# The first scan's convolution as four diagonal matrix products, with a longer ring of row tiles and later stores

## The chip, the core and the metric

The kernel runs on one core of a Trainium2 chip. The core has five engines that run side by side and meet at semaphores: TensorE (PE in the profile; its weight loads are shown apart as PEld), VectorE (DVE), ScalarE (ACT), GpSimd (POOL) and SyncE (SP), which here issues DMAs. Each engine works through its own instruction stream in order. The metric is the device time of one execution, in microseconds (us); lower is better. Three executions of the kernel before took 3533.27, 3534.64 and 3535.41 us, median 3534.64.

## What is computed

The input is 32 sequences of 256 tokens with 256 channels. The result is `x + ffn(cond(x))`: a selective scan, then two layers of local attention and a gated feed-forward. The change lies in `cond`. Cut to what matters:

```python
xr, gate = split(x @ W_in.T)                       # 512 channels each
xr = xr + t_emb[:, None, :]
xc = depthwise_conv(xr, W_conv, 4 taps, 3 zeros in front) + b_conv
xc = silu(xc)
xn = layernorm(xc) * ln_g + ln_b
Bm, Cm, dt = split(xn @ W_xproj.T)
dt = tanh(dt @ W_dt.T + b_dt) * 0.01
Ad, Bd = 1 - dt * tanh(A_log), Bm * min(norm(xn), 1)
for t in range(256):                               # the scan
    h = clip(h * Ad[t] + Bd[t] * xn[t], -10, 10)   # 16 states x 512 channels
    y[t] = Ct[t] . h
return (y + D * xn) * silu(gate) @ W_out.T
```

Each of the 512 channels is convolved with four taps of its own: `xc[c, t] = sum over k of W_conv[c, k] * xr[c, t + k - 3]`.

## The kernel before

The 32 sequences go through in four groups of eight. A group's scan holds its state in a tile of 128 partitions (16 states x 8 sequences) by 512 channels, and takes 256 steps in eight chunks of 32. The scan of group 0 runs by itself (`alone` in the code); those of groups 1 to 3 run beside the attention and feed-forward of the group before. The program between is one long interleaving.

**A step** (L715) is one VectorE instruction: the new state `h` is the old one plus the row `xrep`, clipped. Before it, `scale_row` (L704) multiplies the row by `beta` on ScalarE, and before that the row has to be there, copied to all 16 states. That is done in two ways. For 24 of 32 rows `load_rows` (L684) issues a DMA on SP, 256 KB, from a DRAM copy of the normalised activations (`xnd`). For the other eight (`by_tensor`, two of every eight steps) `spread_rows` (L689) makes it on TensorE (`bx`) from a tile `xq`, which `load_skip` (L738) loads. Both kinds end in a tile of the pool `xp`, tag `xrep`, six buffers. The read-out `y` (L725) is a product on TensorE for each step; four steps write four separate quarters of the same bank.

**The convolution** of the next chunk runs around the start of the current one, for each of four blocks of 128 channels. `project` (L397) forms `ps_in` on TensorE. `conv_in` (L462) adds the condition on VectorE and so writes `xr`, with three tokens carried over from the chunk before in front (runs of 35 for each sequence), and starts the sum `acc` on GpSimd (L480, the first tap and the bias). `conv_taps` (L488) adds three more taps on VectorE (L491). `conv_th` (L496) applies Silu on ScalarE in the first scan; in the later scans tanh is used and `conv_out` finishes it on VectorE. Then follow `raw_sums` (L517), the transposition (`norm_turn`), the norm and `norm_out` (L591), which stores `xn` to `xnd`.

**Beside the first scan** TensorE also projects the inputs of groups 1 to 3: 48 units `ps_a` (`ahead_project`, L423), copied by ScalarE and stored by `ahead_put` (L442), to be read back by the later scans. The weights of the first layer are loaded in this time as well.

**Order.** Each piece of work is entered in an agenda with `at(slot, function, ...)`, where slot `c * 32 + t` is that of step `t` of chunk `c`; `scan_slots` (L935) emits the slots in order, and within one slot first the entries before `agendas.append({})` (L896), then those after it. The framework then writes each engine's stream at compile time: what was emitted first has precedence, but an instruction that isn't ready in its model lets later ones pass. So a stream isn't strictly in slot order: the first weight load of the first layer, emitted in slot 100, is issued at 18.90 us, long before the first step. Once written, a stream is worked through in order.

The slots that matter here, `s0` being the first slot of a chunk: `conv_in` at `s0 - 38 + 2 ch`, `conv_taps` one and `conv_th` two slots later; `norm_out` at `s0 - 17` and `s0 - 13`; `load_skip` at `s0 - 9` and `s0 + 7`; `load_rows` six slots, `spread_rows` four and `scale_row` two ahead of the step.

Of the kernel before, what the change touches and what calls it, by code (L numbers as in the profile page):

```python
# [10 lines left out]
FP = mybir.dt.float32  # L11
BF = mybir.dt.bfloat16
I32 = mybir.dt.int32
AF = mybir.ActivationFunctionType
ALU = mybir.AluOpType
# [4 lines left out]
P = 128  # L20
# [3 lines left out]
DI = 512  # L24
NC_ = DI // P
NS = 16
GB = 8
CH = 32
# [7 lines left out]
TAPS = 4  # L36
# [37 lines left out]
def kernel(  # L74
# [29 lines left out]
    nc = tc.nc  # L104
# [33 lines left out]
    wc_sb = loaded(w_conv, [P, NC_, TAPS], "wc_sb")  # L138
    bconv_sb = loaded(b_conv, [P, NC_], "bconv_sb")
# [5 lines left out]
    ident = const.tile([P, P], FP, tag="ident", name="ident")  # L145
# [17 lines left out]
    for j in range(NJ):  # L163
# [20 lines left out]
        out=mask_t[:, 0:W], in_=mask_t[:, 0:W], compare_op=ALU.is_ge, fill=MASKED_LOW,  # L184
# [3 lines left out]
        out=mask_t[:, W : 2 * W], in_=mask_t[:, W : 2 * W], compare_op=ALU.is_ge,  # L188
# [35 lines left out]
    def program(ctx, exact):  # L224
# [11 lines left out]
        def bank(pool, tag, name):  # L236
            return pool.tile([P, DI], FP, tag=tag, name=name)
# [141 lines left out]
        def group_scan(g):  # L379
# [14 lines left out]
            def at(s, what, *args):  # L394
                agendas[-1].setdefault(s, []).append(partial(what, *args))
# [66 lines left out]
            def conv_in(c, ch):  # L462
                if ch == 0:
                    ck[c]["carry"] = sm.tile(
                        [P, NC_, GB, TAPS - 1], FP, tag="carry", name="carry"
                    )
                    ck[c]["xc"] = sp.tile([P, NC_, GB * CH], FP, tag="xc", name="xc")
                ps = ck[c].pop(("ps", ch))
                xr = sp.tile([P, GB, TAPS - 1 + CH], FP, tag="xr", name="xr", bufs=2)
                if c == 0:  # L470
                    nc.gpsimd.memset(xr[:, :, 0 : TAPS - 1], 0.0)
                else:
                    nc.gpsimd.tensor_copy(xr[:, :, 0 : TAPS - 1], ck[c - 1]["carry"][:, ch])
                nc.vector.tensor_add(
                    xr[:, :, TAPS - 1 :],
                    ps.rearrange("p (b t) -> p b t", b=GB),
                    bc(cond_sb[:, ch, b0 : b0 + GB], 2, CH),
                )
                acc = sp.tile([P, GB, CH], FP, tag="acc", name="acc", bufs=2)
                nc.gpsimd.tensor_scalar(  # L480
                    acc, xr[:, :, 0:CH], wc_sb[:, ch, 0:1], bconv_sb[:, ch : ch + 1],
                    ALU.mult, ALU.add,
                )
                if c < NCH - 1:
                    nc.gpsimd.tensor_copy(ck[c]["carry"][:, ch], xr[:, :, CH:])
                ck[c]["xr", ch] = xr, acc

            def conv_taps(c, ch):  # L488
                xr, acc = ck[c]["xr", ch]
# [6 lines left out]
            def conv_th(c, ch):  # L496
                acc = ck[c]["xr", ch][1]
                if alone:

                    ck[c].pop(("xr", ch))  # L500
                    nc.scalar.activation(
                        ck[c]["xc"][:, ch], acc.rearrange("p b t -> p (b t)"), AF.Silu
                    )
                    return
                th = sp.tile([P, GB * CH], FP, tag="th", name="th", bufs=2)
                nc.scalar.activation(th, acc.rearrange("p b t -> p (b t)"), AF.Tanh, scale=0.5)
                ck[c]["th", ch] = th
# [81 lines left out]
                nc.gpsimd.tensor_add(xn, xn, lnb_sb)  # L589

            def norm_out(c, j):  # L591
                xn = ck[c].pop(("xn", j))
                nc.sync.dma_start(out=ck[c]["xnd"][j * P : (j + 1) * P], in_=xn)
                sq = sp.tile([P, DI], BF, tag="th", name="sq_x", bufs=2)
                nc.scalar.activation(
                    sq, xn, AF.Square, accum_out=ck[c]["ss"][:, j : j + 1]
                )

            def length(c):
# [81 lines left out]
            def by_tensor(t):  # L681
                return alone and t % (2 * NQ) < XR

            def load_rows(c, t):  # L684
                xr = xp.tile([P, DI], FP, tag="xrep", name="xrep")
                ck[c]["rep", t] = xr
                nc.sync.dma_start(out=xr, in_=bc(rows(c)[:, t, :], 0, NS))

# [14 lines left out]

            def scale_row(c, t):  # L704
                if by_tensor(t):
                    ck[c]["rep", t] = xp.tile([P, DI], FP, tag="xrep", name="xrep")
                bx = ck[c]["rep", t]
                scaled = nc.scalar.activation(  # L708
                    bx, ck[c].pop(("bx", t), bx), AF.Copy, scale=ck[c]["beta"][:, t : t + 1]
                )  # L710
                if not alone:

                    tc.keep_in_program_order(scaled)
# [136 lines left out]
            rep_w = []  # L850
            at(-1, start)
            if alone:
                at(-30, spread_weights)
                constants(at)
            for c in range(NCH):
# [2 lines left out]
            for c in range(NCH):  # L858
                s0 = c * CH
                for hb in range(CH // TB):  # L860
                    s = s0 + hb * TB
                    for i in range(NI):
                        at(s + 4 * i + 5, read_out, c, hb, i)
                    at(s + 21, gated, c, hb)
                    at(s + 25, out_gate, c, hb)
                    at(s + 11, skip, c, hb)
                for ch in range(NC_):
                    at(s0 - 38 + 2 * ch, conv_in, c, ch)
                    at(s0 - 37 + 2 * ch, conv_taps, c, ch)
                    at(s0 - 36 + 2 * ch, conv_th, c, ch)  # L870
                    if not alone:
                        at(s0 - 35 + 2 * ch, conv_out, c, ch)
                for ch, s in enumerate((13, 16, 17, 18)):
                    at(s0 + s + 2, gate_th, c, ch)
                    if not alone:
                        at(s0 + s + 4, gate_out, c, ch)
                at(s0 - 25, raw_copy, c)
                at(s0 - 24, raw_turn, c)
                for j in range(NJ):
                    s = s0 - 26 + 4 * j  # L880
                    at(s + 2, norm_stats, c, j)
                    at(s + 5, norm_shift, c, j)
                    at(s + 5, norm_apply, c, j)
                    at(s + 6, norm_affine, c, j)
                    at(s + 9, norm_out, c, j)
                at(s0 - 11, length, c)
                at(s0 - 9, figures, c)
                at(s0 - 7, figures_in, c)
                at(s0 - 6, decay_th, c)
                at(s0 - 5, decays, c)  # L890
                at(s0 - 4, put_c, c, 0)
                at(s0 + 4, put_c, c, 1)
                for d in range(KM):
                    at(s0 + 45 + 2 * d, copy_y, c, d)
                    at(s0 + 46 + 2 * d, put_y, c, d)
            agendas.append({})  # L896
            for c in range(NCH):
                s0 = c * CH
                at(s0 - 43 if alone else s0 + 6, load_x, c)
                if alone:  # L900
                    for ch in range(NC_):
                        at(s0 - 40 + 2 * ch, project, c, ch)
                else:
                    for i in range(2):
                        at(s0 - 44 + 2 * i, load_projected, c, i)
                for ch, s in enumerate((13, 16, 17, 18)):
                    at(s0 + s, project, c, NC_ + ch)
                at(s0 - 27, raw_sums, c)
                for j in range(NJ):
                    at(s0 - 26 + 4 * j, norm_turn, c, j)  # L910
                at(s0 - 8, figures_out, c)
                for t in range(CH):
                    if not by_tensor(t):
                        at(s0 + t - 6, load_rows, c, t)
                    if by_tensor(t) and t % XR == 0:
                        at(s0 + t - 4, spread_rows, c, t)
                    at(s0 + t - 2, scale_row, c, t)
                for hb in range(CH // TB):
                    s = s0 + hb * TB
                    at(s - 9 if alone else s + 7, load_skip, c, hb)  # L920
                    at(s + 23, out_turn, c)
                for d in range(KM):
                    at(s0 + 43 + 2 * d, project_y, c, d)

            if alone:
                n = (NG - 1) * NCH * 2
                for u in range(n):
                    s = -30 + u * (NCH * CH) // n
                    at(s - 5, ahead_load, u)
                    at(s, ahead_project, u)  # L930
                    at(s + 2, ahead_copy, u)
                    at(s + 4, ahead_put, u)
            return agendas

        def scan_slots(groups):  # L935
# [758 lines left out]
```

## Time and profile before

| | |
|---|---|
| median of three runs | 3534.64 us |
| profiled execution: its own time / its span | 3538.39 / 3536.6 us |
| busy over the span: PE, DVE, ACT, POOL | 3415.9, 2682.6, 2031.8, 1625.6 us |
| first step of the first scan | 48.7 us |
| first attention product (L991) | 471.3 us |
| mean granted TensorE clock | 0.992 |

The profile is one execution recorded by the hardware. A row of a group gives line, engine and operation, output and inputs with their shapes, the number of instructions, then busy time in us and the mean of one in ns, and last the idle time of the engine just before them with what ended it. A row of a wait gives who waited for whom, us in total, how many times, and the longest. A row of the timeline gives start, duration, engine, line, operation and, in brackets, the idle time before it. Names are those of the program's tiles; L491 is line 491. Busy times of one group are a union, so that instructions side by side are not counted twice, while means are from each instruction's start to its modelled end.

### The profile page before, as it was taken

The page shows a single profiled execution, that of the slowest core. Times are in us where ns is not written, and L with a number is a line of the kernel's source. Part 1 is how long each engine was busy: PE and PEld are TensorE (multiplying, and loading weights), DVE is VectorE, ACT ScalarE, POOL GpSimd, SP SyncE. Part 2 cuts the span into 40 slices and gives each one's busy share as a digit, 9 for nine tenths or more (in the row PEclk, how much of TensorE's full clock was granted, in tenths as well). Part 3 has the DMA queues.
Part 4 walks back from the last instruction along what each step waited for, and adds up shares of the span by engine and source line. Part 5 has one row for each costly group of instructions (what it writes and reads, how often), then busy time and mean ns, then how long its engine had stood idle before and what let it go on. Part 6 is the DMA issues. An engine that isn't in the chain of part 4 may idle for free.

```text
span 3536.6 us, 56518 instructions
## 1 busy us (share of the span) xinstructions
PE 3415.9 (97%) x19580; PEld 2255.2 (64%) x19580; DVE 2682.6 (76%) x5177; ACT 2031.8 (57%) x3663; POOL 1625.6 (46%) x1587
## 2 busy tenths in 40 slices
PE   7999989999999999999999999999999999999999
PEld 4545335666666666666666666666666777777777
DVE  5888898878787778888888888888787655555563
ACT  4666656666666665666656665666566444444442
POOL 4433456544454555544455455544444434333441
PEclk9999999999999999999999999999999999999999
DMA  7787765544455545444354555444444212011111
GB/s 206 215 218 217 199 172 149 137 115 137 132 138 137 155 141 149 137 115 139 115 143 124 150 145 149 135 118 129 121 140 119 62 37 62 13 31 36 37 28 38
DMA packets 487195, 436.65 MB, mean 123 GB/s; under 512 B 247155, under 2 KB 326516, under 8 KB 486772
## 3 DMA queue, kind: packets, MB, share of 16 engines
q1 hardware_dynamic: 402450, 420.94, 42.2%
q10 hardware_dynamic: 84450, 12.01, 2.1%
q8 instruction: 157, 2.57, 0.3%
q14 instruction: 138, 1.13, 0.1%
HBM read 384.06 MB, written 47.19 MB: 122 GB/s over the span
## 4 chain that ended last, share of the span: by engine, by line
PE 60%; DVE 18%; DMA 8%; POOL 5%; ACT 5%; issue 3%; SPq 0%; ACTq 0%; DVEq 0%; POOLq 0%
PE ps_qkv L991 13%; PE pa L1402 13%; DVE h L718 7%; PE po_f L1429 6%; DMA xrep<-xnd 5%; PE ps_wo L1047 4%; PE y L730 4%; PE ov L1282 3%; PE sc L1227 3%; PE ps_out L810 3%; PE ps_in L401 2%; PE tr_qk L1036 2%; DVE acc L491 2%; PE rs L1264 2%; PE ps_raw L520 2%
## 5 line engine op out<-in xcount | busy, mean ns | idle before, releaser
L718 DVE CUSTOM_DVE_ANT_0 h<-h,xrep,lim 128x512 f32<-128x512 f32 x1024 | 916.7, 895 | 148.1 <-ACT xrep L708 104.4
L708 ACT ACTIVATE xrep<-xrep,beta 128x512 f32<-128x512 f32 x960 | 672.8, 720 | 292.0 <-DMA xrep<-xnd 192.3
L991 PE MATMUL ps_qkv<-qkv,res 128*128 128x512 f32 x1536 | 715.1, 601 | 20.3 <-DVE xd L781 9.5
L1402 PE MATMUL pa<-hT,w 128*128 128x256 f32 (+1 forms) x2816 | 674.3, 382 | 6.0 <-DVE zT L801 6.0
L1402 PEld LDWEIGHTS pa<-hT,w 128*128 128x128 f32 (+1 forms) x2816 | 517.0, 188 | 146.1 <-issue 42.4
L1015 POOL TENSOR_TENSOR rot<-rot,swp 128x512 f32<-128x512 f32 x256 | 346.1, 1352 | 496.4 <-DVE swp L1012 462.0
L991 PEld LDWEIGHTS ps_qkv<-qkv,res 128*128 128x128 f32 x1536 | 281.7, 191 | 304.3 <-issue 246.8
L1021 POOL TENSOR_TENSOR rn<-ss,neg_half 128x8 f32<-128x8 f32 x256 | 458.9, 1793 | 0.0
L730 PE MATMUL y<-h,ly 128*32 128x512 f32 x2048 | 343.8, 606 | 16.3 <-DVE h L718 14.3
L1429 PE MATMUL po_f<-ag,w 128*128 128x256 f32 x1280 | 307.2, 387 | 3.9 <-DVE fo L1440 2.8
L1420 DVE SCALAR_TENSOR_TENSOR ag<-pa,b_sb,ag 128x256 f32<-128x256 f32 x320 | 151.3, 473 | 204.9 <-ACT ag L1413 204.8
L1429 PEld LDWEIGHTS po_f<-ag,w 128*128 128x128 f32 x1280 | 235.8, 190 | 68.3 <-DVE pT L1255 12.9
L1004 ACT ACTIVATE sq<-ps_qkv,tiny 128x512 f32<-128x512 f32 x256 | 172.2, 685 | 178.2 <-PE ps_qkv L991 118.7
L1413 ACT ACTIVATE ag<-pa,b_sb 128x256 f32<-128x256 f32 x320 | 150.3, 470 | 208.9 <-PE pa L1402 205.9
L1354 POOL TENSOR_TENSOR rstd<-ve,neg_half 128x2 f32<-128x2 f32 x64 | 46.2, 722 | 484.9 <-DVE ve L1352 484.9
L1047 PE MATMUL ps_wo<-oT,wo 128*128 128x256 f32 x1024 | 231.6, 379 | 0.0
L1007 DVE TENSOR_TENSOR rot<-ps_qkv,rc_sb 128x512 f32<-128x512 f32 x256 | 174.2, 680 | 67.4 <-ACT sq L1004 65.8
L491 DVE SCALAR_TENSOR_TENSOR acc<-xr,wc_sb,acc 128x256 f32<-128x256 f32 x384 | 184.8, 503 | 49.0 <-POOL acc L480 48.3
L1012 DVE TENSOR_TENSOR swp<-ps_qkv,rs_sb 128x256 f32<-128x256 f32 x512 | 191.8, 416 | 27.6 <-POOL rot L1015 27.5
L1047 PEld LDWEIGHTS ps_wo<-oT,wo 128*128 128x128 f32 x1024 | 194.5, 190 | 27.2 <-ACT xrep L708 0.8
L1239 ACT ACTIVATE pT<-sc 128x512 f32<-128x512 f32 x384 | 201.7, 601 | 14.8 <-PE sc L1227 12.7
L1227 PE MATMUL sc<-qT,kT 64*128 64x128 f32 (+2 forms) x2304 | 197.6, 331 | 12.6 <-DVE swp L1012 8.8
(161 smaller groups left out, 5379.1 us busy)
## 6 DMA issues: line engine op xcount, KB each, us to landing
xrep<-xnd SPq DMA_DIRECT2D x960, 256.0 KB
rb<-inv SPq DMA_DIRECT2D x128, 256.0 KB
xnd<-xn SPq DMA_DIRECT2D x64, 256.0 KB
qkv<-in_wqkv_dram SPq DMA_DIRECT2D x24, 512.0 KB
ahead<-xs_a SPq DMA_DIRECT2D x48, 256.0 KB
xp<-ahead SPq DMA_DIRECT2D x48, 256.0 KB
xd<-xnd SPq DMA_DIRECT2D x192, 64.0 KB
w<-in_w_dram SPq DMA_DIRECT2D x80, 128.0 KB
```

Source lines behind the costliest of these rows:

```text
L491: nc.vector.scalar_tensor_tensor(acc, xr[:, :, k : k + CH], wc_sb[:, ch, k : k + 1], acc, ALU.mult, ALU.add,)
L708: scaled = nc.scalar.activation(bx, ck[c].pop(("bx", t), bx), AF.Copy, scale=ck[c]["beta"][:, t : t + 1])
L718: nc.vector._custom_dve(TENSOR_ADD_SAT, out=h_new, in0=state["h"], in1=bx, s0=ck[c]["lim"][:, 0, t : t + 1], s1=ck[c]["lim"][:, 1, t : t + 1],
L730: nc.tensor.matmul(ck[c]["y", hb][32 * q : 32 * q + 32, :], ly[hb % 2][:, 32 * t : 32 * t + 32], ck[c].pop(("h", hb * TB + t)), start=(i = ...
L991: nc.tensor.matmul(ps, res[b][:, k, t0 : t0 + W], wt["qkv", a][:, k], start=(k == 0), stop=(k == KM - 1),)
L1015: nc.gpsimd.tensor_add(rot, rot, swp)
L1021: nc.gpsimd.tensor_tensor(rn, ss, neg_half, ALU.pow)
L1047: nc.tensor.matmul(po[:, d], wt["wo", 0][:, c, d * P : (d + 1) * P], oT[:, c, :], start=(c == 0), stop=(c == NC_ - 1),)
L1227: nc.tensor.matmul(banks[r][k0 : k0 + mk, i, q0:q1], kT[rows, i0 + i, kw * W + k0 : kw * W + k0 + mk], qT[rows, i0 + i, kw * W + q0 : kw * ...
L1239: nc.scalar.activation(p, banks[r], AF.Exp)
L1402: nc.tensor.matmul(dst[x], wt["w1", m][:, k, x], self.h[:, k], start=(k == 0), stop=(k == KM - 1),)
L1429: nc.tensor.matmul(self.po[:, d], wt["w2", 0][:, m, d * P : (d + 1) * P], self.ag[m], start=(m == 0), stop=(m == len(MCH) - 1),)
```

## The change

It has four parts, all for the first scan (`alone`) of the usual branch of the program.

1. The sum `acc` on GpSimd and the three taps on VectorE are dropped. At the start `taps_diagonal` writes for each block of channels and each tap a 128 x 128 matrix with the tap's weights on its diagonal (16 ScalarE activations of the identity with a scale for each partition). `conv_products` then forms the convolution as four accumulating products on TensorE in a PSUM bank, with `xr` shifted by one token as the moving operand, one slot after `conv_in`. The Silu reads that bank and adds the bias.
2. The rows' tiles come from a ring of ten: six of `xp` and four in tiles that the attention uses later (`qT`, `kT`, `rb`, `v`). The diagonals lie in such tiles too (`oT`, `hn`, `hT`).
3. `load_rows` is entered eight slots ahead of the step, not six.
4. The store of `xn` is parted from `norm_out` (`norm_put`) and entered two slots later; the store of a projected half (`ahead_put`) four slots later.

```diff
-                acc = sp.tile([P, GB, CH], FP, tag="acc", name="acc", bufs=2)
-                nc.gpsimd.tensor_scalar(
-                    acc, xr[:, :, 0:CH], wc_sb[:, ch, 0:1], bconv_sb[:, ch : ch + 1],
-                    ALU.mult, ALU.add,
-                )
+                acc = None
+                if not alone:
...
+            def taps_diagonal(ch):
+                if ch == 0:
+                    t = ap_.tile([P, 2, TAPS, P], FP, tag="oT", name="taps", bufs=1)
+                    state["taps", 0], state["taps", 1] = t[:, 0], t[:, 1]
+                elif ch > 1:
+                    state["taps", ch] = ap_.tile(
+                        [P, TAPS, P], FP, tag=("hn", "hT")[ch - 2], name="taps", bufs=1
+                    )
+                for k in range(TAPS):
+                    nc.scalar.activation(
+                        state["taps", ch][:, k], ident, AF.Copy, scale=wc_sb[:, ch, k : k + 1]
+                    )
+
+            def conv_products(c, ch):
+                xr, _ = ck[c]["xr", ch]
+                ps = bank(ps_w, "w", "cv")[:, 0 : GB * CH]
+                for k in range(TAPS):
+                    nc.tensor.matmul(
+                        ps.rearrange("p (b t) -> p b t", b=GB),
+                        state["taps", ch][:, k],
+                        xr[:, :, k : k + CH],
+                        start=(k == 0),
+                        stop=(k == TAPS - 1),
+                    )
+                ck[c]["xr", ch] = xr, ps
...
-                        ck[c]["xc"][:, ch], acc.rearrange("p b t -> p (b t)"), AF.Silu
+                        ck[c]["xc"][:, ch], acc, AF.Silu, bias=bconv_sb[:, ch : ch + 1]
...
+            def norm_put(c, j):
+                nc.sync.dma_start(
+                    out=ck[c]["xnd"][j * P : (j + 1) * P], in_=ck[c].pop(("xn", j))
                 )
...
+            def row_tile():
+
+                n = state["rows"] = (state.get("rows", -1) + 1) % (6 if exact else 10)
+                if not alone or n < 6:
+                    return xp.tile([P, DI], FP, tag="xrep", name="xrep")
+                tag = ("qT", "kT", "rb", "v")[n - 6]
+                t = ap_.tile(
+                    [P, 2, DI], FP, tag=tag, name="xrep", bufs=2 if tag == "v" else 1
+                )
+                return t[:, 0]
...
+                for ch in range(NC_):
+                    at(-41 + ch, taps_diagonal, ch)
...
-                    at(s0 - 37 + 2 * ch, conv_taps, c, ch)
+                    if not alone:
+                        at(s0 - 37 + 2 * ch, conv_taps, c, ch)
...
+                    at(s + (11 if alone else 9), norm_put, c, j)
...
+                        at(s0 - 37 + 2 * ch, conv_products, c, ch)
...
-                        at(s0 + t - 6, load_rows, c, t)
+                        at(s0 + t - (8 if alone and not exact else 6), load_rows, c, t)
...
-                    at(s + 4, ahead_put, u)
+                    at(s + 8, ahead_put, u)
```

`load_rows` and `scale_row` take their tile from `row_tile()` instead of the pool.

More of the change, by code (lines that the diff above doesn't have):

```diff
@@ L478, in conv_in @@
                 )
-                acc = sp.tile([P, GB, CH], FP, tag="acc", name="acc", bufs=2)
-                nc.gpsimd.tensor_scalar(
-                    acc, xr[:, :, 0:CH], wc_sb[:, ch, 0:1], bconv_sb[:, ch : ch + 1],
-                    ALU.mult, ALU.add,
-                )
+                acc = None
+                if not alone:
+                    acc = sp.tile([P, GB, CH], FP, tag="acc", name="acc", bufs=2)
+                    nc.gpsimd.tensor_scalar(
+                        acc, xr[:, :, 0:CH], wc_sb[:, ch, 0:1], bconv_sb[:, ch : ch + 1],
+                        ALU.mult, ALU.add,
+                    )
                 if c < NCH - 1:
@@ L591, in norm_out @@
             def norm_out(c, j):
-                xn = ck[c].pop(("xn", j))
-                nc.sync.dma_start(out=ck[c]["xnd"][j * P : (j + 1) * P], in_=xn)
+                xn = ck[c]["xn", j]
                 sq = sp.tile([P, DI], BF, tag="th", name="sq_x", bufs=2)
@@ L596, in norm_out @@
                     sq, xn, AF.Square, accum_out=ck[c]["ss"][:, j : j + 1]
+                )
+            def norm_put(c, j):
+                nc.sync.dma_start(
+                    out=ck[c]["xnd"][j * P : (j + 1) * P], in_=ck[c].pop(("xn", j))
                 )
@@ L682, in by_tensor @@
                 return alone and t % (2 * NQ) < XR
+            def row_tile():
[5 more added lines that the diff above has]
+                    [P, 2, DI], FP, tag=tag, name="xrep", bufs=2 if tag == "v" else 1
+                )
+                return t[:, 0]
             def load_rows(c, t):
-                xr = xp.tile([P, DI], FP, tag="xrep", name="xrep")
+                xr = row_tile()
                 ck[c]["rep", t] = xr
@@ L705, in scale_row @@
                 if by_tensor(t):
-                    ck[c]["rep", t] = xp.tile([P, DI], FP, tag="xrep", name="xrep")
+                    ck[c]["rep", t] = row_tile()
                 bx = ck[c]["rep", t]
```

## The prediction

> **What bounds the first scan.** The change touches the first scan alone: head (0 to 48 us), scan proper, then a mixed stage from about 471 us in which TensorE is never short of work (295.0 of 300 us busy between 600 and 900 us, clock 1.00). What the first scan saves or costs is therefore passed on to the end one for one, and I looked there only. I read first busy time by stretch, one row per chunk of 32 steps (columns: stretch, its length, busy us of PE, PEld, DVE, ACT, POOL, then the granted clock, DMA share, GB/s):
>
> ```profile
> 96.00:145.00 49.00, 44.45 (x203) 25.52 (x203) 43.43 (x76) 31.87 (x58) 21.13 (x29) 0.98 0.80 220
> 145.00:193.00 48.00, 44.89 (x201) 23.70 (x201) 41.98 (x72) 30.67 (x59) 19.80 (x26) 0.96 0.79 216
> 193.00:242.00 49.00, 45.72 (x204) 24.66 (x203) 40.91 (x74) 31.48 (x58) 17.93 (x25) 0.95 0.81 222
> 48.00:387.00 339.00, 316.85 (x1403) 171.81 (x1402) 287.59 (x503) 219.30 (x404) 132.27 (x173) 0.96 0.80 216
> ```
>
> A chunk takes some 48.4 us, in which TensorE is busy 45 us, VectorE 42 us and the DMA engines 80%. None is idle enough to be ignored. Next, the groups of instructions in the seven chunks between 48 and 387 us:
>
> ```profile
> L718 DVE CUSTOM_DVE_ANT_0 h<-h,xrep,lim 128x512 f32<-128x512 f32 x221 | 207.3, 938 | 27.9 <-ACT xrep L708 18.7 <-DVE h L718 2.0 <-PE y L730 0.3
> L428 PE MATMUL ps_a<-xa,w_in_sb 128*128 128x256 f32 x344 | 92.0, 413 | 3.6 <-DMA xa<-in_xT_dram 3.6
> L730 PE MATMUL y<-h,ly 128*32 128x512 f32 x441 | 84.0, 606 | 2.6 <-DVE h L718 2.5
> L401 PE MATMUL ps_in<-xg,w_in_sb 128*128 128x256 f32 x216 | 60.2, 413 | 2.4 <-DMA xg<-in_xT_dram 2.2 <-ACT xrep L708 0.2
> L491 DVE SCALAR_TENSOR_TENSOR acc<-xr,wc_sb,acc 128x256 f32<-128x256 f32 x81 | 40.6, 501 | 8.1 <-POOL acc L480 8.1
> L480 POOL TENSOR_SCALAR acc<-xr,wc_sb,bconv_sb 128x256 f32<-128x256 f32 x28 | 28.2, 1008 | 59.1 <-DVE xr L474 56.3 <-ACT xs_a L439 2.0 <-ACT xrep L708 0.8
> ```
>
> L491 and L480 are what goes. The means of the PE rows (413 ns) are latencies; what a matmul costs in a queue is read from TensorE's timeline, from start to start:
>
> ```profile
> 143.85 3.20 PE L428 MATMUL ps_a<-xa,w_in_sb 128*128 128x256 f32 x8
> 150.21 1.99 PE L428 MATMUL ps_a<-xa,w_in_sb 128*128 128x256 f32 x8
> 152.13 1.13 PE L695 MATMUL bx<-xq,rep_w 32*128 32x512 f32 x4
> 153.19 1.05 PE L730 MATMUL y<-h,ly 128*32 128x512 f32 x4
> ...
> 154.71 1.04 PE L730 MATMUL y<-h,ly 128*32 128x512 f32 x2 [0.47 <-DVE h L718]
> ...
> 172.00 1.89 PE L401 MATMUL ps_in<-xg,w_in_sb 128*128 128x256 f32 x8
> 173.82 1.07 PE L730 MATMUL y<-h,ly 128*32 128x512 f32 x8
> 174.81 1.99 PE L401 MATMUL ps_in<-xg,w_in_sb 128*128 128x256 f32 x8
> ```
>
> One call of a 128x128x256 product leaves two records, so x8 is four calls: 1.82 to 1.92 us from start to start, 1.86 in the mean. Four read-outs y cost 1.0 us when they run side by side (x8) and 1.0 us for each lot when split (x4, x2). At 143.85 the same eight records took 3.20 us: a low clock after a stop.
>
> **Where TensorE stops**, waits in the same 339 us:
>
> ```profile
> PE bx L695 <- ACT xrep L708: 6.2, 3, 2.4
> PE bx L695 <- DMA xq<-xnd: 4.9, 4, 1.8
> PE ps_a L428 <- DMA xa<-in_xT_dram: 3.6, 4, 1.3
> PE ps_st L620 <- DVE rhs L611: 2.5, 4, 0.9
> SPq L687 <- DVE h L718: 42.2, 49, 3.9
> SPq L593 <- POOL xn L589: 6.0, 6, 2.2
> ```
>
> The stops sit at the chunk boundaries. At 188.5 us ScalarE has stood 3.67 us for a row whose load SP had issued only at 183.4; the decay's activation behind it came late, VectorE waited 2.0 us for that, TensorE 1.9 us for the bank of bx.
>
> **Part 1, the convolution leaves VectorE and GpSimd.** In the 339 us 81 L491 go, 40.6 us, and their 8.1 us of waiting for L480: VectorE needs 239 us instead of 288. That alone would allow 339 - 48.7 = 290 us if nothing else were late. GpSimd loses 28 us. L718's mean is 938 ns against a minimum of 785, because it lengthens beside GpSimd's passes (1.70 us at 208.88 beside L760); L480 is one of these passes. I put no gain on it (0 to 3 us).
>
> **Part 2, it comes to TensorE.** Four calls per channel and chunk, the shape of L401: 1.86 us for each of 27 channel-chunks in the stage (81/3) = 50.2 us. That xr is read in runs of 32 out of 35 isn't shown by a row of this shape; between 0 and +10% I take 0, since weights and columns are those of L401. Weight loads overlap (25 of 48 us busy). ScalarE's 32 Silu keep their cost (L501: 412 ns; bound -0.05 to +0.2 us each when read from PSUM, L439's copy of 512 columns takes 0.58). Sixteen diagonals on ScalarE: 128x128 lies between L645 (128x32, 0.31 us) and L501 (0.41), 5 to 7 us, in the first 10 us, where ScalarE is busy 1.5 us. The first xr is ready at 12.8 us; cost 0, and up to 3 us if they delay the weight DMAs that ScalarE issues.
>
> The stage's ledger for TensorE, by counts and starts: ps_a 43 x 1.87 = 80.4, ps_in 27 x 1.83 = 49.4, y 55 x 1.0 = 55, bx 28.5 x 1.06 = 30.2, ps_out 12 x 1.88 = 22.6, ps_raw 14, transposes 13.3, ps_st 3.5: 268.4 us. The other 70.6 of 339 us are: idle 22.2; 29 for split y (84.0 - 55); 12.7 for the clock (4% of 316.9); 7 left over. With the convolution the ledger is 318.6, so TensorE becomes the bound, and the result hangs on how much of the 70.6 survives.
>
> A rule stands against that reading. The Trainium skill (Perfetto Trace Analysis, Identifying the Most-Contended Engine) holds that TensorE's headroom isn't judged by matmul busy time but by the weight loads' busy share. That is 51% here (171.8 of 339) and would leave ample room, so that VectorE's 290 us would count: -49 us. The row decides otherwise: from 161 to 183 us TensorE's matmuls start without a gap at the very spacing that the bound needs, and the sum of spacings is 79% of the stage. I take the row.
>
> **Part 3, ring of ten and loads two slots earlier.** A load waited for the step six rows back, of its own slot (42.2 us of SP's waiting on L718). Now the tile is that of ten rows back, stepped two slots before. Two slots are 3.0 us, which covers most of the 3.67 us stop. So bx<-ACT (6.2) goes, and with it low clock. For the clock the skill (TensorE: Matmul & The Clock Gate, Why this matters for your kernels) warns of gaps over some 3 us; the gaps here are 1.9 and 2.4 us, so that by the rule nothing is lost now, yet the row shows 0.66 between 190 and 200 us. By the rule 0 us is to be regained, by the row 12.7; I take the row. DMA share would be 0.82 at the forecast length: no bound (slices of 0.99 occur), but more loads stand in front of xq, whose lateness (4.9 us) I keep.
>
> **Part 4, stores later.** xnd's store loses its place before two slots of row loads and ahead's before four; SP's waits for them (6.0 and, for xs_a, 11.8 us) stop blocking loads. Readers: xq two slots later. The stores preceded the xq loads by 8.0 us (226.57 to 234.62), so 3 us less is covered; without that cover each of seven boundaries would cost up to 3 us. The projected halves are read from slot 212, far behind.
>
> **Sum.** When TensorE is always behind, y come in fours and it stops rarely: between 600 and 900 us it idles 1.7% at clock 1.00, and y cost 1.19 us per four. Full batching gives 0, that row 10.5 us; I take 4, since here all of TensorE's work is queued. Of the 7 left over I keep 4. (318.6 + 8)/0.983 = 332 us, **-7** against 339 (ends: 324 with nothing kept, 373 with 54 of the 70.6 kept). After 387 us neither convolution is on TensorE; ScalarE waits 13.9 us for rows in that chunk but L718 hardly for ScalarE: -3 (-6 to +1). Head: 0 (-2 to +3). Total -10 on the profiled span, 3536.6 to 3526.6; that run took 3538.39, the runs' median is 3534.64, so **3525 us**; own range 3510 to 3533.
>
> **Rivals.** *Wash*: y at 1.19 us and all 7 kept: (318.6 + 17.5)/0.983 = 342, +3 - 3: 3535 us. For it: that is the only saturated row there is. *Slower*: the diagonal products wait on TensorE. They stand at the boundary, each behind its xr addition, which VectorE does between steps; the spread rows bx stand behind them in order, and the steps behind bx; ScalarE's Silu now waits for TensorE too, with the row scalings behind it. At 0.9 us a channel, 27 x 0.9 = 24 us on a full engine, plus 10 for y left split: +34 - 10 = 3559 us. It decides from about 0.4 us a channel. For it: L474 came 2 us after its ps_in at 188.1; against it: three slots (4.5 us) lie between. *VectorE was all*: the weight loads' reading is right, 3534.6 - 49 = 3486 us.
>
> **Chances.** A change under 0.2% (7 us) can't be told from none. Forecast 0.42 (0.06 of it within 7 us), wash 0.20 (0.16 within, 0.04 above), slower 0.30, VectorE 0.08. Faster 0.44, same 0.22, slower 0.34. Range 3504 to 3560 leaves out the last rival and the worst of the slower one.
>
> **What would show it.** Chunk rows with PE above 46 us and clock 0.99; L730 under 70 us in the stage; no bx<-ACT waits; VectorE near 36 us a chunk and now idle for TensorE. The forecast is wrong if conv products show PE waits on xr, if y stays split, or if chunks pass 49 us.

## The result: slower by 0.9%

The kernel after takes 3569.05 us (median of four runs, 3565.50 to 3572.34) beside 3533.95 us for the kernel before in the same rounds: a ratio of 1.0092, 95% interval 1.0076 to 1.0107. The forecast was 3525 us, range 3504 to 3560. The profiled execution has a span of 3570.6 us, 34.0 more than the profile of before. From its page, busy time by engine, share of the span, and instructions:

```profile
PE 3458.3 (97%) x19836; PEld 2302.3 (64%) x19836; DVE 2638.8 (74%) x5081; ACT 2036.8 (57%) x3679; POOL 1601.8 (45%) x1555
```

VectorE has lost 44 us of work and GpSimd 24, TensorE has gained 42. Where the 34 us arose is seen by marking the first scan's steps (counted from 0 in the traces; columns in us):

| | first step | step 224 | the seven chunks between | first attention product |
|---|---|---|---|---|
| before | 48.7 | 392.4 | 343.7 | 471.3 |
| after | 53.7 | 425.5 | 371.8 | 502.7 |

The head costs 5.0 us more (in the kernels below the first step falls anywhere between 45.1 and 58.6 us, in no clear order with their edits, so I read nothing from it), the seven chunks 28.1 more, the last chunk up to the attention 1.7 less, and all that follows 2.6 more of 3065. The loss lies in the seven chunks. The stretches of after, three of 50 us and last the one of all seven chunks (length, busy us of PE, PEld, DVE, ACT, POOL, granted clock, DMA share, GB/s):

```profile
98.00:148.00 50.00, 46.97 (x227) 28.41 (x225) 32.10 (x52) 30.00 (x54) 16.67 (x22) 0.93 0.76 198
148.00:198.00 50.00, 46.12 (x228) 28.30 (x224) 32.75 (x57) 31.48 (x58) 18.05 (x23) 1.00 0.73 194
198.00:248.00 50.00, 48.37 (x232) 29.22 (x232) 33.46 (x59) 28.98 (x54) 15.16 (x21) 0.97 0.76 200
53.70:425.50 371.80, 347.81 (x1623) 207.18 (x1621) 247.04 (x435) 224.54 (x411) 113.81 (x152) 0.96 0.75 200
```

A chunk now takes 53.1 us. VectorE fell from 42 us to 35 of every chunk (247.0 over seven), as wanted. TensorE is busy 347.8 us of 371.8: 24.0 idle, no fewer than before (22.3 of 343.7), and the clock is still 0.96. The groups of the same stretch:

```profile
L761 DVE CUSTOM_DVE_ANT_0 h<-h,xrep,lim 128x512 f32<-128x512 f32 x224 | 195.3, 872 | 93.0 <-ACT xrep L751 60.4 <-PE y L773 15.2 <-PE tp_x L578 4.7
L428 PE MATMUL ps_a<-xa,w_in_sb 128*128 128x256 f32 x343 | 89.0, 406 | 0.4 <-ACT sg L373 0.4
L773 PE MATMUL y<-h,ly 128*32 128x512 f32 x448 | 69.9, 631 | 4.4 <-DVE h L761 4.4
L507 PE MATMUL cv<-xr,taps 128*128 128x256 f32 x216 | 52.5, 385 | 1.6 <-DVE xr L474 1.6
L529 ACT ACTIVATE xc<-cv,bconv_sb 128x256 f32<-128x256 f32 x27 | 12.2, 460 | 7.0 <-PE cv L507 7.0
```

L507 is the convolution: 27 channel-chunks, 52.5 us, and it hardly waits for its xr (1.6 us). The step L761 now stands idle 93.0 us before its 224 instructions, where it stood 27.9 before 221. Who waits for whom in the stretch (us in total, times, longest):

```profile
ACT xrep L751 <- DMA xrep<-xnd: 105.6, 65, 6.3
DVE h L761 <- ACT xrep L751: 60.4, 24, 5.3
DVE h L761 <- PE y L773: 15.2, 9, 4.6
PE ps_out L853 <- DVE mv L590: 7.1, 6, 2.6
PE cv L507 <- DVE xr L474: 1.6, 2, 1.3
```

ScalarE's own waiting for rows from the DMA was 71.7 us before. The stops of TensorE on bx behind ScalarE's rows are gone from the list, but others have come (ps_out behind the layer norm's figures, 7.1 us). SyncE's queue in the same stretch:

```profile
SPq L627 <- POOL xn L617: 35.0, 13, 4.5
SPq L730 <- DVE h L761: 34.4, 45, 3.7
SPq L444 <- ACT xs_a L439: 31.5, 15, 5.8
```

The two stores (L627, L444) that were to stop blocking SyncE block it for 66.5 us, against 17.8 before (11.8 and 6.0). One such place in the timeline of after:

```profile
162.87 4.05 SPq L730 DMA_DIRECT2D xrep<-xnd  x4
...
166.86 0.72 ACT L751 ACTIVATE xrep<-xrep,beta 128x512 f32<-128x512 f32 x1 [1.99 <-DMA xrep<-xnd]
...
169.53 0.72 ACT L751 ACTIVATE xrep<-xrep,beta 128x512 f32<-128x512 f32 x1 [0.98 <-DMA xrep<-xnd]
...
170.52 0.57 ACT L439 COPY xs_a<-ps_a 128x512 f32<-128x512 f32 x1
...
171.12 0.34 SPq L444 DMA_DIRECT2D ahead<-xs_a  x1
171.57 0.73 ACT L751 ACTIVATE xrep<-xrep,beta 128x512 f32<-128x512 f32 x1
171.72 0.81 DVE L761 CUSTOM_DVE_ANT_0 h<-h,xrep,lim 128x512 f32<-128x512 f32 x1 [5.35 <-ACT xrep L751]
...
174.28 1.47 SPq L730 DMA_DIRECT2D xrep<-xnd  x2
```

After its four row loads SyncE stands before the store of xs_a until ScalarE has made the copy, at 171.1. That copy is behind row scalings on ScalarE, which wait for rows, which SyncE loads. The step waits 5.35 us, and the next rows are asked for only at 174.3.

### The profile page after: what moved, and what is told of

It is laid out like the page before. It is cut to its first block, busy times and chain, and to the rows that moved or that the text cites. A ratio compares the mean times of both kernels' runs of the same rounds, so it can differ in the third digit from the quotient of the medians.

```text
span 3570.6 us, 56907 instructions
## 1 busy us (share of the span) xinstructions
PE 3458.3 (97%) x19836; PEld 2302.3 (64%) x19836; DVE 2638.8 (74%) x5081; ACT 2036.8 (57%) x3679; POOL 1601.8 (45%) x1555
## 4 chain that ended last, share of the span: by engine, by line
PE 62%; DVE 18%; DMA 8%; POOL 5%; ACT 4%; issue 3%; SPq 1%; ACTq 0%; DVEq 0%; POOLq 0%
PE ps_qkv L1039 13%; PE pa L1450 12%; DVE h L761 7%; PE po_f L1477 6%; DMA xrep<-xnd 5%; PE ps_wo L1095 4%; PE y L773 4%; PE ov L1330 3%; PE ps_out L853 3%; PE ps_in L401 3%; PE sc L1275 3%; PE tr_qk L1084 2%; PE rs L1312 2%; DVE acc L519 2%; DMA xp<-ahead 1%
## 5 line engine op out<-in xcount | busy, mean ns | idle before, releaser
L761 DVE CUSTOM_DVE_ANT_0 h<-h,xrep,lim 128x512 f32<-128x512 f32 x1024 | 905.3, 884 | 214.0 <-ACT xrep L751 146.8
L773 PE MATMUL y<-h,ly 128*32 128x512 f32 x2048 | 326.1, 611 | 16.0 <-DVE h L761 15.3
L1060 DVE TENSOR_TENSOR swp<-ps_qkv,rs_sb 128x256 f32<-128x256 f32 x512 | 191.7, 416 | 28.5 <-POOL rot L1063 28.4
L1075 DVE SCALAR_TENSOR_TENSOR rot<-rn,rot 128x512 f32<-128x512 f32 x256 | 204.9, 838 | 7.5 <-POOL rn L1069 7.5
```

Of the source, the lines that this page charges most:

```text
L761: nc.vector._custom_dve(TENSOR_ADD_SAT, out=h_new, in0=state["h"], in1=bx, s0=ck[c]["lim"][:, 0, t : t + 1], s1=ck[c]["lim"][:, 1, t : t + 1],
L773: nc.tensor.matmul(ck[c]["y", hb][32 * q : 32 * q + 32, :], ly[hb % 2][:, 32 * t : 32 * t + 32], ck[c].pop(("h", hb * TB + t)), start=(i = ...
L1075: nc.vector.scalar_tensor_tensor(rot, bc(rn, 2, DH), 1e12, rot, ALU.min, ALU.mult)
```

## The experiments

All ratios are to the kernel before on the same chip, in the same rounds. The theories that the quoted expectations weigh: TensorE has become the bound, by the work added; the rows come late, since SyncE or the ring holds them up; the state's ring of eight, which holds the step up until y has read it; and, with each, whether the parts of the change pull apart.

No run changes one thing alone, since the framework writes the streams anew for every kernel. Of the instructions that two kernels share in the seven chunks (those of the edited work left out), this many stand in the same order: after and one tap, 402 of 425 on VectorE and 275 of 371 on ScalarE; before and before with halved `ps_a`, 354 of 426 and 294 of 369. TensorE's read-outs stand in 69 lots in before, 57 in after, 60 with one tap and 92 in before with halved `ps_a`. What a new order is worth by itself wasn't measured. Differences of 0.2 to 0.3% below may be in part of that kind; those of about 1% have several runs behind them.

**The parts apart.** The convolution alone, with the old ring, lead and stores:

```diff
-                n = state["rows"] = (state.get("rows", -1) + 1) % (6 if exact else 10)
+                n = state["rows"] = (state.get("rows", -1) + 1) % 6
...
-                        at(s0 + t - (8 if alone and not exact else 6), load_rows, c, t)
+                        at(s0 + t - 6, load_rows, c, t)
...
-                    at(s + (11 if alone else 9), norm_put, c, j)
+                    at(s + 9, norm_put, c, j)
...
-                    at(s + 8, ahead_put, u)
+                    at(s + 4, ahead_put, u)
```

> The convolution on TensorE alone; ring of six, loads six slots ahead and stores where they stood. Theory A (SP stands behind stores that wait for late results, so rows come late): the stores stand in front of even more row loads than in the changed kernel, so slower than it, 3575 to 3600 us. Theory B (TensorE is full, its added 50 us set the time): the same TensorE work, so the same as the changed kernel within 6 us, 3563 to 3575 us.

Measured 1.0101 (1.0084 to 1.0118). And the rest alone, with the convolution put back on VectorE and GpSimd:

```diff
-                        at(s0 - 37 + 2 * ch, conv_products, c, ch)
...
+                    at(s0 - 37 + 2 * ch, conv_taps, c, ch)
```

> Ring of ten, earlier loads and later stores alone; the convolution as before on GpSimd and VectorE. Theory A: rows come earlier and SP waits less for the stores, 3505 to 3525 us. Theory B: TensorE as before, its waits for ScalarE at the chunk boundaries gone, 3524 to 3534 us. If parts 3 and 4 themselves do harm: above 3540 us.

Measured 1.0002 (0.9988 to 1.0015). The whole loss is the convolution's, and the ring, the earlier loads and the later stores bring nothing by themselves. With it they may take back 0.1%, which these intervals don't separate from none. SyncE's waits for the two stores in the seven chunks tell more. In the convolution alone, with the stores in their old places:

```profile
SPq L444 <- ACT xs_a L439: 65.8, 29, 7.1
SPq L627 <- POOL xn L617: 31.0, 14, 3.8
```

That is 96.8 us, against 66.5 in the kernel after and, without the convolution on TensorE, 6.3 (0.8 and 5.5), where the kernel before had 17.8. So the later stores did relieve the queue, and the convolution blocked it again.

**Less work for TensorE, the rest unchanged.** One of the four products per channel is issued; three taps are left out of the computation:

```diff
-                for k in range(TAPS):
+                for k in range(1):
...
-                        stop=(k == TAPS - 1),
+                        stop=(k == 1 - 1),
```

> The changed kernel with one of the four diagonal products per channel and chunk; three taps of the convolution are left out, and with them 38 us of TensorE's work in the stage and 12 of 16 diagonals aren't read. Theory B: 38 us less on a full engine, 3528 to 3538 us. Theory A: the late results come somewhat earlier, but the stores still stand in SP's way: 3548 to 3562 us.

Measured 0.9979 (0.9971 to 0.9987): 44.6 us fewer on TensorE (32 x 3 products of 0.465) give back 1.13%, 40 us. To see whether the place of the work matters, the same 44.6 us were taken elsewhere in the kernel after, from the projection ahead, where half of the contraction is left out:

```diff
-                    for k in range(KM):
+                    for k in range(1):
...
-                            stop=(k == KM - 1),
+                            stop=(k == 0),
```

> The changed kernel with half of the contraction left out of the projection of the later groups' inputs (ps_a): 96 calls, 44.6 us of TensorE's work that no step of the first scan waits for. Theory B: any 44.6 us count, 35 to 45 us less than the changed kernel, ratio to before 0.997 to 0.999. Theory D (the diagonal products cost by where they stand, in front of bx and y): 10 to 20 us less, 1.004 to 1.006.

Measured 0.9988 (0.9979 to 0.9997), 37 us less than after. Not the place counts, but the sum, as far as two cuts can tell. The same cut in the kernel before:

> The kernel before with the same half of ps_a left out. If TensorE set the pace of the first scan before the change as well: 30 to 45 us less, ratio 0.987 to 0.992. If VectorE did: 0 to 10 us less, 0.997 to 1.000.

Measured 1.0035 (1.0017 to 1.0053): no gain, and somewhat slower, for a reason that the trace doesn't settle (the steps waited 31.4 us for ScalarE's rows against 18.0; of the 16.8 us by which the profiled span is longer, 8.4 lie in the head; and the streams stand in another order). It agrees with a kernel before that TensorE did not bind, but doesn't prove it by itself. First before, then the kernel before with the cut, same stretch and columns as above:

```profile
53.70:400.00 346.30, 323.59 (x1422) 170.86 (x1420) 296.06 (x521) 223.60 (x411) 135.97 (x179) 0.97 0.79 215
```

```profile
53.70:400.00 346.30, 318.67 (x1223) 140.21 (x1224) 281.75 (x505) 218.05 (x401) 135.04 (x176) 0.97 0.77 209
```

199 records fewer, and the busy time falls by 5 us only. The read-outs fill the room, first before, then with the cut:

```profile
L730 PE MATMUL y<-h,ly 128*32 128x512 f32 x458 | 92.4, 606 | 3.2 <-DVE h L718 3.0
```

```profile
L730 PE MATMUL y<-h,ly 128*32 128x512 f32 x438 | 129.7, 618 | 7.7 <-DVE h L718 7.1
```

No more of them, at the same mean, cover 37 us more of the time: 219 calls at 0.59 us each, which is one by one, where before many ran side by side. In the seven chunks 42 of the 69 lots of before hold four calls, and 27 of 92 with the cut. As the stream's order is fixed at compile time, this lies in the program as written, so the cut changed more than the sum of the work. Busy time of TensorE is no measure of how much it has left.

**No convolution on any engine.** Silu reads xr itself; all four taps are left out:

```diff
-                        ck[c]["xc"][:, ch], acc, AF.Silu, bias=bconv_sb[:, ch : ch + 1]
+                        ck[c]["xc"][:, ch].rearrange("p (b t) -> p b t", b=GB),
+                        xr_[:, :, TAPS - 1 :], AF.Silu, bias=bconv_sb[:, ch : ch + 1]
...
-                        at(s0 - 37 + 2 * ch, conv_products, c, ch)
```

> The changed kernel with the first scan's convolution left out altogether: Silu reads xr itself. It shows what VectorE's and GpSimd's relief is worth when TensorE pays nothing. From one tap (0.9979) and four (1.0092) on a straight line: 0.994, some 21 us less than before, for 48 us of VectorE's work. If VectorE was the bound before: 0.988 or less.

Measured 0.9946 (0.9930 to 0.9963). This splits the result in two: taking the convolution off VectorE and GpSimd is worth 0.54%, 19 us; giving it to TensorE costs 1.46%, 52 us. The first 14.9 us of it (one tap) cost 12 us already.

**What holds the rows and the state up.** The kernel after with both stores on ScalarE's queue, and the old slots or earlier:

```diff
-                nc.sync.dma_start(out=d, in_=state.pop(("ta", u)))
+                nc.scalar.dma_start(out=d, in_=state.pop(("ta", u)))
...
-                    at(s + 8, ahead_put, u)
+                    at(s + 3, ahead_put, u)
```

(the store of xn likewise, at s + 9)

> The changed kernel, but in the first scan both stores (normalised rows and projected halves) are issued by ScalarE, which makes or reads the data anyway, and not by SP. Theory A: SP no longer waits for xn and xs_a (69 us of waits between 48 and 400 us), rows are early, VectorE's 60 us of waiting for scaled rows fall under 25: 3530 to 3548 us. Theory B: TensorE's work is unchanged, 3560 us or more.

Measured 1.0064 (1.0045 to 1.0083). Its waits of VectorE up to 400 us:

```profile
DVE h L761 <- ACT xrep L751: 64.3, 31, 8.0
DVE h L761 <- PE y L773: 15.0, 10, 2.4
```

SyncE's largest wait is now for steps that free a row tile (95.2 us in the seven chunks), 10 us are won, and the steps wait for their rows as long as ever: the blocked queue is at most a part of the loss. The state's ring from eight tiles to twelve, with six for the rows and their loads six slots ahead, since the same four tiles serve only one ring:

```diff
-                h_new = hp.tile([P, DI], FP, tag="h", name="h")
+                n = state["hs"] = (state.get("hs", -1) + 1) % (8 if exact else 12)
+                if not alone or n < 8:
+                    h_new = hp.tile([P, DI], FP, tag="h", name="h")
+                else:
+                    tag = ("qT", "kT", "rb", "v")[n - 8]
...
```

> The convolution on TensorE and the later stores, row ring of six with loads six slots ahead; the four attention tiles go to the states h instead, a ring of twelve for eight. Theory C (VectorE's 15 us of waiting for the read-outs y are waits for a free state tile: TensorE's lag reaches the steps after eight of them): 10 to 15 us under the convolution alone, ratio to before 1.005 to 1.007. Theory B (TensorE is full, whoever waits for it): as the convolution alone, 1.009 to 1.011.

Measured 1.0069 (1.0052 to 1.0087). The waits of VectorE in it:

```profile
DVE h L768 <- ACT xrep L751: 88.4, 59, 5.8
DVE ad L682 <- ACT ad L677: 9.5, 5, 2.1
```

The waits for y are gone, and those for rows take their place. Some 0.2% against after, or 0.3% against the convolution alone, is in it, and the kernel stays slower than before.

**More work for TensorE.** The four products issued twice:

```diff
-                for k in range(TAPS):
+                for k in 2 * list(range(TAPS)):
```

> The kernel after with each convolution's four products issued twice (the second four start the sum anew, so the result is the same): 32 x 1.86 = 59.5 us more for TensorE, 50 of it in the stage. TensorE full: the slope of the first four products goes on, 0.88 to 1 us per us, a ratio of 1.024 to 1.026. Rows or the state's turn bound the kernel after: below 1.016.

Measured 1.0190 (1.0176 to 1.0204), between what the two expected. 59.5 us more cost 35 us, 0.58 us per us, where one tap to four had cost 0.90. Its read-outs and products up to 400 us, and one lot of products in its timeline:

```profile
L507 PE MATMUL cv<-xr,taps 128*128 128x256 f32 x396 | 94.6, 392 | 11.4 <-DVE xr L474 10.8 <-DVE ad L682 0.7
L773 PE MATMUL y<-h,ly 128*32 128x512 f32 x368 | 51.2, 613 | 2.6 <-ACT sg L373 2.6
```

```profile
228.55 3.70 PE L507 MATMUL cv<-xr,taps 128*128 128x256 f32 x16 [1.48 <-DVE xr L474]
```

Eight calls in 3.70 us: xr's runs of 32 out of 35 cost nothing. The read-outs come side by side (54 of 57 lots in the seven chunks hold four calls), as they do in after, where it is 54 of 57 too. Its seven chunks as a whole:

```profile
58.57:466.18 407.61, 382.20 (x1841) 241.88 (x1840) 247.02 (x436) 228.27 (x413) 116.48 (x152) 0.98 0.70 182
```

The clock is at 0.98, and still TensorE is idle for 25.4 us. Even twice the convolution doesn't bring about the 1.7% of idling on which the forecast built.

**A smaller dose.** If VectorE bounds the one side and TensorE the other, a part of the convolution may pay. One of the four channel blocks goes to TensorE, three stay:

```diff
-                        at(s0 - 37 + 2 * ch, conv_products, c, ch)
+                        if ch == 0:
+                            at(s0 - 37 + 2 * ch, conv_products, c, ch)
...
-                    if not alone:
+                    if not alone or ch > 0:
                         at(s0 - 37 + 2 * ch, conv_taps, c, ch)
```

> The kernel after with only the first of a chunk's four channel blocks convolved on TensorE; the other three keep GpSimd's first tap and VectorE's three. Two-bound theory: VectorE with GpSimd allows 3534 us with all their convolution and gains up to 1 us per us taken off them (48 us in all), TensorE allows 3519 us without any convolution (the run with none, 0.9946) and loses 0.88 us per us added (59.5 us in all). A quarter gives VectorE 3534 - 12 = 3522 and TensorE 3519 + 13 = 3532: the later decides, a ratio of 0.998 to 1.000, no gain. Rival, the place of the products hurts and not their sum: a quarter of the loss at the most, 1.002 to 1.003. If TensorE still had room for a first part: the relief alone, 0.9965.

Measured 1.0016 (1.0007 to 1.0024): above what the theory of two bounds allowed; the interval reaches into what the place of the products would cost. The same with both stores issued by ScalarE, as above:

> The same quarter, with both stores (the projection ahead and the normalised block) issued by ScalarE three and nine slots after their step and not by SyncE. For the kernel after this was worth 0.28% (1.0092 to 1.0064). If the stores' blocking of the row loads costs time of its own, the same here: 0.995 to 0.998, faster than before and after both. If it only counted where TensorE was late, 0.998 to 1.000.

Measured 0.9952 (0.9938 to 0.9965): faster than before and after. And those stores alone, in the kernel before:

> The kernel before with nothing changed but the queue of those two stores: issued by ScalarE, one slot earlier and behind the square. Blocking costs time of its own: 0.996 to 0.998. It is hidden in the kernel before, as the run with the later stores and the ring but the old convolution (1.0002) says: 0.999 to 1.002.

Measured 1.0008 (0.9999 to 1.0017): nothing that can be told from none. The waits of SyncE in the quarter kernel up to 400 us, and in the same kernel with ScalarE's stores:

```profile
SPq L735 <- DVE h L766: 26.2, 35, 2.5
SPq L632 <- POOL xn L622: 22.2, 9, 3.6
SPq L735 <- DVE acc L519: 12.9, 17, 2.6
SPq L444 <- ACT xs_a L439: 9.7, 9, 2.5
```

```profile
SPq L735 <- DVE h L766: 76.3, 61, 6.7
SPq L795 <- DMA xnd<-xn: 11.2, 6, 3.7
```

In the second SyncE waits above all for one thing, the step that frees a row tile, which means that it is ahead of the rows' use; in the first it stands before stores. VectorE's waiting for rows falls from 24.8 to 12.1 us with it, and TensorE's clock in the stage of after (columns as before) goes from 0.95, first row, to 0.99:

```profile
53.70:425.50 371.80, 340.28 (x1523) 183.69 (x1522) 301.42 (x531) 233.60 (x432) 146.23 (x182) 0.95 0.80 207
```

```profile
53.70:425.50 371.80, 345.85 (x1575) 181.78 (x1573) 322.16 (x570) 243.99 (x456) 155.86 (x195) 0.99 0.83 217
```

Taking the stores off SyncE is worth nothing in before, 0.3% in after, 0.6% in the quarter kernel. My reading, not shown by a run, is that the blocking costs where an engine beside it has been given room that it then can't use. Not tried: half of the convolution with these stores; the ring of ten with them but without any product; and the kernel before with products added for TensorE and its own convolution left where it was, which would have measured the price of the work by itself.

## Why the prediction was wrong

The step that failed is the **Sum**. TensorE's ledger demanded 318.6 us with the convolution, and the forecast let little survive on top: some 13.4 us, for 332. Measured are 371.8: **53.2 us survived**, of the 70.6. Term by term:

| | forecast | measured in the seven chunks |
|---|---|---|
| TensorE idle | 5.6 (1.7% of 332) | 24.0 (371.8 - 347.8) |
| low clock | 0 | 13.9 (4% of 347.8) |
| read-outs beyond 1.0 us for four, and left over | 8 (4 and 4) | 15.3 (the rest of 53.2) |

The step took it that TensorE, once always behind, would rarely stop and run at full clock. It stood still for 6.5% of the stretch and ran at 0.96: 37.9 us of the 53.2 are idle time and low clock, which the forecast put at 5.6. The batching of the read-outs, which it expected, did come: 54 of 57 lots hold four calls, where before 42 of 69 did. What makes up the 15.3 isn't told apart.

The high end that the forecast named for itself, 373 with 54 kept, is what came. Here are the seven chunks of all runs beside TensorE's demand in them by the prediction's prices and counts (268.4 without products, 12.55 for each quarter of them, 40 off where ps_a is halved):

| | demand | seven chunks | what is left | of it, TensorE idle | ratio |
|---|---|---|---|---|---|
| before, halved ps_a | 228.4 | 350.4 | 122.0 | 27.4 | 1.0035 |
| before | 268.4 | 343.7 | 75.3 | 22.3 | 1 |
| before, ScalarE's stores | 268.4 | 346.6 | 78.2 | 18.6 | 1.0008 |
| ring, loads and stores alone | 268.4 | 340.7 | 72.3 | 22.5 | 1.0002 |
| no convolution | 268.4 | 332.5 | 64.1 | 27.6 | 0.9946 |
| after, halved ps_a | 278.6 | 337.7 | 59.1 | 28.4 | 0.9988 |
| one tap | 281.0 | 341.1 | 60.1 | 32.7 | 0.9979 |
| quarter | 281.0 | 349.1 | 68.1 | 31.4 | 1.0016 |
| quarter, ScalarE's stores | 281.0 | 327.2 | 46.2 | 22.2 | 0.9952 |
| after, ScalarE's stores | 318.6 | 364.9 | 46.3 | 29.8 | 1.0064 |
| after, state ring of twelve | 318.6 | 367.2 | 48.6 | 33.8 | 1.0069 |
| after | 318.6 | 371.8 | 53.2 | 24.0 | 1.0092 |
| convolution alone | 318.6 | 384.3 | 65.7 | 38.2 | 1.0101 |
| products twice | 368.8 | 407.6 | 38.8 | 25.4 | 1.0190 |

A row is one execution, and the runs used several chips, on which the median of the kernel before was 3533.95, 3537.37, 3546.53 and 3546.77 us; so I read nothing from differences of under some 10 us between rows.

What is left never falls below 38.8 us, and idle time never below 18.6, even with 50 us more of work in the queue. The forecast took the survival from the stage between 600 and 900 us, the only saturated one in the trace. There 104 steps of the next scan fall into 300 us, among the products of the attention; here 224 fall into 372, and read-outs, rows and output products in TensorE's queue stand behind a state, a row or a layer norm that VectorE, ScalarE and SyncE must deliver first. That this difference is the reason is argued and not shown. The runs show no single wait that holds the rest: taking one away (y's, or the stores') gives back 0.2 to 0.3%. Why so much survives stays open in part.

By its other steps:
- **Part 1**: VectorE's relief was as sized, its worth wasn't. Of the 49 us that VectorE alone would allow, the run without any convolution has 19. VectorE's groups in the rows before didn't show that the rest of the loop would be next so soon. (The shortest L718 in those 339 us takes 790 ns and not 785; nothing hangs on it.)
- **Part 2**: the price of the products was right (1.86 us per channel and chunk; 3.70 for two lots), so were Silu (460 ns against 412) and the diagonals (16 of 387 ns). The rule of the Trainium skill (Perfetto Trace Analysis, Identifying the Most-Contended Engine) is right that TensorE's matmul busy time doesn't tell its headroom: with half of ps_a gone it fell only from 93% to 92%. The weight loads' share doesn't tell here either: 51% before and 56% after (207.18 of 371.8), where 44.6 us of work less are worth 37 to 40. The page names the share of peak arithmetic (MFU) beside it, which the prediction left out and no run here gives. The -49 us don't come even where TensorE gets nothing.
- **Part 3**: the waits of bx on ScalarE went, as forecast, the low clock did not: 0.96 before and after. The stops moved to other places. This is the term of the clock in the table above, 12.7 us given up that were kept.
- **Part 4**: alone, the later stores did what was forecast (17.8 us of waiting became 6.3, with the ring and the earlier loads), and it was worth nothing. What was overlooked is that the convolution on TensorE makes the stores' producers late: 96.8 us with the stores in their old places, 66.5 in the later ones.
- **Tail**: -3 forecast, -1.7 measured up to the attention, within its range.
- **Slower**, the rival, had the sign and nearly the size (3559). The trace of after refutes both of its terms: TensorE idles 1.6 us for xr, not 24 (in the convolution alone 9.6), and the read-outs aren't split.
- **Its own signs** misled. TensorE came to 49.7 us a chunk (above 46), y to 69.9 (under 70), VectorE to 35.3 (near 36), and bx no longer waited for ScalarE's rows: four of the signs of a gain, in a kernel that lost. VectorE idled less for TensorE (15.2 us on y) than for ScalarE's rows (60.4). Only this, the clock and the length of a chunk, 53.1 us where more than 49 was to refute the forecast, told.

## What to carry to other kernels

Before work is moved from one engine to another, take it off the giver without putting it anywhere: the run without any convolution (0.9946) puts the gain at 0.54%, and such a run can be had before the move is built. Cutting the receiver's work is no such test: here it gave nothing (1.0035), which looks like room, and yet the products cost 1.46%. Measure the price by adding work to the receiver, as the run with the products issued twice did for the kernel after.

In a loop that passes through four engines at every step, don't plan an engine at its net demand as if its idle and slow time went away when work is added. Here 59.5 us of products on a kernel without them cost 52 us, and as many again 35. And a small dose with the queue in front of it cleared (a quarter, with the stores on another queue) gained 0.5% where the whole lost 0.9%.

## What the runs showed of the hardware

A stop of TensorE of some 3 us can be followed by a longer stretch at about half speed. In the timeline of the run with one tap:

```profile
195.83 1.89 PE L428 MATMUL ps_a<-xa,w_in_sb 128*128 128x256 f32 x8
197.66 1.07 PE L773 MATMUL y<-h,ly 128*32 128x512 f32 x8
...
202.58 3.75 PE L853 MATMUL ps_out<-zT,w_out_sb 128*128 128x256 f32 x8 [3.27 <-DVE mv L590]
...
206.26 2.08 PE L738 MATMUL bx<-xq,rep_w 32*128 32x512 f32 x4
...
208.27 3.70 PE L428 MATMUL ps_a<-xa,w_in_sb 128*128 128x256 f32 x8
211.90 1.06 PE L773 MATMUL y<-h,ly 128*32 128x512 f32 x8
212.89 1.99 PE L853 MATMUL ps_out<-zT,w_out_sb 128*128 128x256 f32 x8
```

ps_out takes 3.75 us and ps_a 3.70, where ps_a took 1.9 before the stop; the granted clock from 202.6 to 212.6 us is 0.54. By 211.9 the speed is back. The stop cost 3.3 us and the slow 9 us after it some 4.7 more.

It isn't always so. In the fourteen traces TensorE's matmuls stop 24 times for 2.3 us or more between 50 and 430 us. In the 10 us after, the granted clock is between 0.54 and 0.85 in 22 cases, and 1.00 in two (after 3.13 us in the kernel before with halved ps_a, after 2.34 us in the kernel before with ScalarE's stores). Shorter stops go either way: 0.66 after 1.92 us in before, 1.00 after 2.23 us with the state ring of twelve. Nor does the clock follow the sum of idle time: over their seven chunks it is 0.98 both with the products twice (25.4 us idle) and in the convolution alone (38.2), and 0.96 in after (24.0).
